# One instead of many: biases of an attention block carried by the first channel of the normalised rows, and an output bias moved from TensorE to GpSimd

## The chip, the cores and the metric

The kernel runs on one core of one Trainium2 chip. The metric is the device time of one execution in microseconds (us), the median of several runs. Beside these runs stands one execution under the hardware profiler, from which all durations of single instructions come.

## The reference

The input `x` is (4, 2048, 256) in float32: four sequences of 2048 tokens with 256 channels. Four blocks run one after the other, each on a layer norm (without gain or shift) of the current `x`, each adding its result to `x`:

```
x = x + broadcast over t of (norm(x)[:, 1] @ W.T + b)        # one row for a sequence
x = x + ffn(norm(x))                                           # token shift, W_k, relu^2, W_v, sigmoid gate
x = x + attention(norm(x))                                     # 16 heads of 64, blocks of 128, band mask
x = x + ffn(norm(x))                                           # the same weights as before
```

The attention projects `q`, `k`, `v` as `norm(x) @ W.T + bias`, turns `q` and `k` by their position, lets every block of 128 tokens look at itself and the block before it, and projects the result as `merged @ Wo.T + bo`. The biases `bq`, `bk`, `bv` and `bo` are not zero; they are what the change is about.

## The kernel before

The tokens are cut into 32 groups of 256 (`GB` = 2 blocks of 128), eight groups for each sequence. For each group the steps are: `Load` (load `x`, add the row of the first block), `Ffn` 0, `Ln` (layer norm for the attention, split into two float16 parts, transposed by DMA), `Val` and four `Qk` (projections, four heads at a time), four `Att` (scores, softmax, context), `Out` (output projection, added to `x`), `Ffn` 1, `Store`. Float32 precision is kept by splitting operands in a high and a low part and multiplying three times.

Each step has a line in a `SPEC` table: name, engine (`p` TensorE, `v` VectorE, `s` ScalarE, `g` GpSimd, `q` the DMA queue of SyncE), assumed duration, needed steps, buffers taken and given back. `Plan.order` plays these through with one queue for each engine: among the steps that could begin within `SLACK` (0.3 us) of the earliest, the one of lowest rank goes next. A rank is 44 us times the group plus an entry of the table `RANK` for the kind of step; the first and last five groups have further entries (`x!0`, `ln!-1`). The order so found is the program order of every engine, and an engine runs strictly in it. So a number in `RANK` moves instructions of one engine past each other without changing what they compute.

The places around the change:

- `Stats.scale` (on GpSimd) makes the two columns `rs` of a layer norm from mean and variance. For the attention's `Ln` it takes `shift = var * scale - mean`, so that `(x + shift) * scale` is the norm **plus one in every channel**. `Ln.xn` applies it on GpSimd; `Ln.hi` (ScalarE) and `Ln.lo` (GpSimd) make the two float16 parts.
- `Setup.fetch` builds the projection weights that go with this. The normalised row sums to zero over its channels, so each weight column may be shifted by a constant. Into a PSUM bank of 512 columns go: the matrix `less` (identity minus 1/256) times one half of the weights, `nones` (-1/256) times the other half, and four matmuls of `spread` that add the bias over 256 to every row. So the column sums to the bias, and "norm plus one" times it is the projection with its bias. This runs for q, k and v, for two halves of the channels (`wq0`, `wq1`, ...) and two banks each: 12 banks. `scale`, `hi` and `low` (VectorE, ScalarE, VectorE) then write the two float16 parts of the weights.
- `Setup.ob` (ten small GpSimd instructions) splits `bo` into three bfloat16 rows, `bo3`. In `Out.mm` every output bank half ends with one matmul of `ones` by `bo3`, which adds `bo` to the 24 matmuls of the projection: two for each group, 64 in all. `Out.add` on VectorE adds the bank to `x`.

The small biases are loaded by three DMAs of ScalarE's queue (`lb`); nearly all other DMAs go through SyncE's queue.

Of the kernel before, what the change touches and what calls it, by code (L numbers as in the profile page):

```python
# [8 lines left out]
BF16 = mybir.dt.bfloat16  # L9
# [9 lines left out]
P = 128  # L19
# [32 lines left out]
    "p.c1": -5056.91, "p.c2": 2969.02, "p.c3": -4885.05, "p.lv": -3111.05, "p.lb": -2925.83, "p.lw": -5009.81,  # L52
    "p.lo": -413.49, "p.lk": -2678.25, "p.lm": 2640.67, "p.lq": -3077.55, "p.fk": -1972.19, "p.fr": -2838.78,
    "p.fv": -777.00, "p.bd": -2779.47, "p.nvs": 3014.63, "p.nvm": 3072.90, "p.nvr": -2978.83, "p.nks": -788.22,
    "p.nkm": -4306.80, "p.nkr": -83.63, "p.nqs": -5037.35, "p.nqm": -4939.68, "p.nqr": -774.36, "p.sc": -472.11,
    "p.wv0": 570.16, "p.xv0": -201.89, "p.yv0": 3153.22, "p.zv0": -4686.76, "p.wv1": -2600.05, "p.xv1": -3342.91,
    "p.yv1": -610.29, "p.zv1": -4852.83, "p.wk0": -3021.86, "p.xk0": -1892.46, "p.yk0": -821.64, "p.zk0": -2369.83,
    "p.wk1": -2733.80, "p.xk1": -83.69, "p.yk1": -1953.56, "p.zk1": -2430.55, "p.wq0": -168.05, "p.xq0": 2297.47,
    "p.yq0": -4898.14, "p.zq0": -5081.41, "p.wq1": 2689.14, "p.xq1": -2913.52, "p.yq1": 3363.58, "p.zq1": -5071.63,
    "p.mk": -3071.43, "p.mu": -2906.24, "p.frh": -2530.67, "p.frl": -2423.55, "p.fkh": -2983.12, "p.fkl": 3185.31,  # L60
    "p.fvs": -769.81, "p.fvh": -4579.58, "p.fvl": 3091.15, "p.oq": -3006.79, "p.om": -204.90, "p.oc": -4648.57,
    "p.ox": -4580.42, "p.ob": -4965.08, "p.wo0": -613.03, "p.yo0": -2788.56, "p.zo0": -2882.62, "p.wo1": 3475.98,
    "p.yo1": -4703.07, "p.zo1": -4980.00, "r.ld": -5200.49, "r.st": 3455.58, "r.rs": -4687.73, "r.xn": 3456.91,
    "r.tr": 2907.19, "r.cp": -4814.90, "r.mm": 3513.18, "r.bi": -4976.56, "r.ad": -273.75, "x.ld": -4781.49,
    "x.a1": -513.94, "f0.st": -4882.63, "f0.rs": 2754.65, "f0.xn": 2986.21, "f0.tr": -4910.79, "f0.xt": -4990.79,
    "f0.hs": -3080.33, "f0.d": 2586.18, "f0.xm": -151.13, "f0.xo": -4611.65, "f0.xh": 976.57, "f0.xl": -4986.30,
    "f0.pk": -393.93, "f0.pr": -1868.76, "f0.rl": 3385.50, "f0.sq": 2308.38, "f0.kh": -5040.27, "f0.kl": -676.62,
    "f0.th": -6078.70, "f0.pv": 1034.70, "f0.sg": -4582.52, "f0.ad": 2796.64, "ln.st": -560.18, "ln.rs": -2135.71,
    "ln.xn": -358.88, "ln.hi": -845.47, "ln.lo": -4727.91, "ln.tr": -4597.42, "ln.cs": 1425.54, "tab.sc": 2955.10,
    "tab.st": -4548.65, "v0.mm": 1390.97, "v0.hi": -4851.14, "v0.lo": -952.76, "v1.mm": -2687.29,  # L70
    "v1.hi": -2644.64, "v1.lo": 2842.52, "v2.mm": 75.57, "v2.hi": -351.20, "v2.lo": -3081.42, "v3.mm": -4752.71,
    "v3.hi": -3057.25, "v3.lo": -4482.10, "q0.qm": -697.49, "q0.km": -1950.26, "q0.ka": -2699.89,
    "q0.kb": -5039.26, "q0.ad": 6.08, "q0.hi": -4974.92, "q0.lo": -5211.77, "q0.ks": -630.96, "q1.qm": -3584.31,
    "q1.km": -5189.02, "q1.ke": -5178.75, "q1.ka": -4943.18, "q1.mu": -992.72, "q1.ad": 1417.95, "q1.hi": 2888.04,
    "q1.lo": -4733.64, "q1.ks": -4326.00, "q2.qm": -468.39, "q2.km": -5058.89, "q2.ka": -2789.23,
    "q2.kb": -2972.37, "q2.ad": -2884.86, "q2.hi": 2658.83, "q2.lo": -924.24, "q2.ks": -2518.12, "q3.qm": 518.16,
    "q3.km": -4610.64, "q3.ka": 2530.62, "q3.kb": -4722.76, "q3.ad": -2764.39, "q3.hi": 2839.46, "q3.lo": -857.55,
    "q3.ks": -6086.78, "s0.k0": -1920.73, "s0.k1": -4586.15, "s0.k2": -613.21, "s0.k3": -2474.73,
    "s0.ks": -1923.23, "s0.sc": -3035.71, "s0.m0": -3099.45, "s0.m1": -3049.20, "s0.m2": -3015.22,
    "s0.m3": 2557.63, "s0.e0": -861.34, "s0.h0": -2876.34, "s0.l0": -2849.45, "s0.e1": 3370.73, "s0.h1": -2599.69,  # L80
    "s0.l1": 1349.23, "s0.t0": -2539.64, "s0.e2": 3083.70, "s0.h2": -1860.52, "s0.l2": 3055.36, "s0.e3": 2664.91,
    "s0.h3": -4879.42, "s0.l3": -610.50, "s0.t1": -4583.99, "s0.av": -4852.99, "s0.i0": 570.93, "s0.n0": -3079.20,
    "s0.ch": 2366.40, "s0.cl": -571.44, "s0.tc": -571.05, "s1.k0": -3309.12, "s1.k1": -1922.89, "s1.k2": -3002.20,
    "s1.k3": -2726.33, "s1.ks": -184.97, "s1.sc": -2823.37, "s1.m0": -2407.99, "s1.m1": -5176.15,
    "s1.m2": -1860.79, "s1.m3": 2664.46, "s1.e0": -2792.04, "s1.h0": -5036.68, "s1.l0": -5011.21,
    "s1.e1": -2759.97, "s1.h1": -2211.92, "s1.l1": -435.00, "s1.t0": -901.97, "s1.e2": 3228.18, "s1.h2": -2875.68,
    "s1.l2": -330.17, "s1.e3": -3095.98, "s1.h3": -4480.63, "s1.l3": -2400.51, "s1.t1": -40.32, "s1.av": -4976.07,
    "s1.i0": -302.67, "s1.n0": -5059.03, "s1.ch": -2945.71, "s1.cl": -4833.32, "s1.tc": -580.01, "s2.k0": -5104.06,
    "s2.k1": -2518.92, "s2.k2": -609.18, "s2.k3": -198.65, "s2.ks": -4270.64, "s2.sc": -3396.12, "s2.m0": -5359.90,
    "s2.m1": 3353.04, "s2.m2": -2954.66, "s2.m3": 2954.52, "s2.e0": -4801.17, "s2.h0": -4748.29, "s2.l0": -2533.65,  # L90
    "s2.e1": 2657.60, "s2.h1": -4876.22, "s2.l1": -143.77, "s2.t0": 3181.31, "s2.e2": -4740.23, "s2.h2": -1971.93,
    "s2.l2": -938.59, "s2.e3": 2929.40, "s2.h3": 3383.64, "s2.l3": -3250.26, "s2.t1": -4528.02, "s2.av": -3295.20,
    "s2.i0": -813.73, "s2.n0": -495.95, "s2.ch": -48.33, "s2.cl": 3091.26, "s2.tc": -696.74, "s3.k0": -677.40,
    "s3.k1": -3123.97, "s3.k2": -1933.84, "s3.k3": -465.00, "s3.ks": -4922.97, "s3.sc": -3446.85, "s3.m0": -798.61,
    "s3.m1": -4809.14, "s3.m2": 2876.12, "s3.m3": -4696.24, "s3.e0": -3417.38, "s3.h0": -4927.16,
    "s3.l0": -1999.52, "s3.e1": -4448.94, "s3.h1": -2880.18, "s3.l1": -280.82, "s3.t0": -2938.10,
    "s3.e2": -4878.66, "s3.h2": 3143.56, "s3.l2": -4964.39, "s3.e3": -4936.60, "s3.h3": -2514.89,
    "s3.l3": -1028.30, "s3.t1": -492.35, "s3.av": -2744.89, "s3.i0": 3016.46, "s3.n0": -1868.36, "s3.ch": 884.13,
    "s3.cl": -4564.07, "s3.tc": -5366.32, "o.o0": 2643.02, "o.o1": -3044.73, "o.ad": -158.89, "f1.st": 2937.82,
    "f1.rs": -2889.62, "f1.xn": 3469.38, "f1.tr": -4576.63, "f1.xt": 552.29, "f1.hs": -510.30, "f1.d": -2519.76,  # L100
    "f1.xm": 3150.42, "f1.xo": -608.94, "f1.xh": -2506.38, "f1.xl": -4708.72, "f1.pk": -1296.49, "f1.pr": 3476.81,
    "f1.rl": -5093.90, "f1.sq": -2850.79, "f1.kh": -5039.71, "f1.kl": -814.45, "f1.th": -3076.11, "f1.pv": 2685.28,
    "f1.sg": -2990.66, "f1.ad": -805.51, "sv.sv": -5172.96, "q0.kp": -272.05, "q1.kp": 3376.69, "q2.kp": -1225.68,
    "q3.kp": 3472.01, "o.b0": 1345.63, "o.b1": -2554.79, "w0.sv": 3471.29, "f2.st": -5011.19, "f2.rs": -3308.71,
    "f2.xn": -3405.13, "f2.tr": -2831.72, "f2.xt": -3325.07, "f2.hs": -2014.91, "f2.d": 1332.12, "f2.xm": 2950.21,
    "f2.xo": 2796.33, "f2.xh": 3364.00, "f2.xl": -909.62, "f2.pk": -2992.00, "f2.pr": 2885.42, "f2.rl": 539.64,
    "f2.sq": 1425.59, "f2.kh": -67.86, "f2.kl": 2844.93, "f2.th": 2905.43, "f2.pv": -5337.55, "f2.sg": 3157.44,
    "f2.ad": -4704.62, "w1.sv": 3214.41, "x!0": 280.61, "f0!0": -466.19, "ln!0": -1931.41, "tab!0": 407.32,
    "v0!0": -398.48, "v1!0": -330.74, "v2!0": -346.65, "v3!0": 347.03, "q0!0": -660.79, "q1!0": 28.80,
    "q2!0": 462.27, "q3!0": -379.97, "s0!0": 250.27, "s1!0": 1256.31, "s2!0": 655.38, "s3!0": -1508.73,  # L110
    "o!0": -1757.96, "f1!0": -2364.52, "sv!0": 2125.66, "x!1": -633.85, "f0!1": -1962.50, "ln!1": 1727.42,
    "tab!1": -240.15, "v0!1": -2055.69, "v1!1": -17.38, "v2!1": -1635.07, "v3!1": -1933.31, "q0!1": 1435.50,
    "q1!1": -913.86, "q2!1": 541.01, "q3!1": -1282.06, "s0!1": -1069.83, "s1!1": 856.98, "s2!1": -2363.56,
    "s3!1": -571.61, "o!1": 860.95, "f1!1": 519.89, "sv!1": -1291.03, "x!2": -877.71, "f0!2": -334.58,
# [1582 lines left out]
```

## Time and profile before

| what | value |
|---|---|
| median of three runs | 1602.65 us (1599.9 to 1604.53) |
| the profiled execution, its own time | 1597.72 us |
| span of its instructions | 1595.9 us |
| mean granted TensorE clock | 0.991 |
| instructions | 55776 |
| distance between the first and last output projection (`po`, groups 0 and 31) | 163.6 to 1574.8 us |

A view by groups gives, for each kind of instruction, its engine, output and inputs, the shape, the count, the busy time and the mean of one, and behind the last bar how long the engine was idle just before them and what ended that. A view by windows gives the busy time of every engine in a stretch of the span. The chain is the work that ended last, followed backwards: each piece is an instruction that nothing but the piece before it held up. All instructions carry line 276, the helper that records them, so they are told apart by their tiles: `u_q`, `u_k`, `u_v` are the banks of `fetch`, `po` that of `Out`, `a_*` belongs to `Ln`, `f_*` to `Ffn`, `at_*` to `Att`, `qk_*` to `Qk`. A matmul's duration includes its way through the array: where matmuls follow each other, the distance from start to start is what one costs.

### The profile page before, as it was taken

To read this page: it belongs to the slowest core of one execution; us is meant where nothing else is said; L and a number is where in the kernel's file an instruction comes from. 1 tells how busy PE (TensorE), PEld (TensorE's weight loads), DVE (VectorE), ACT (ScalarE), POOL (GpSimd) and SP (SyncE) were. 2 spreads that over 40 slices of the span, in tenths; PEclk is the share of its full clock that TensorE was granted. 3 is DMA by queue.
4 is the path that set the end of the run, shared out by engine and by line. 5 is a ranking of instruction groups with operands and counts; after the bars stand their busy time and mean duration, and the time that the engine had idled before them with its cause. 6 is when DMAs were issued, how large, how long until landed. Compare 5 with 4: busy or idle time off the path is not lost.

```text
span 1595.9 us, 55776 instructions
## 1 busy us (share of the span) xinstructions
PE 1493.1 (94%) x22887; PEld 1241.3 (78%) x22888; DVE 1438.1 (90%) x2607; ACT 1345.6 (84%) x2742; POOL 1317.3 (83%) x1409
## 2 busy tenths in 40 slices
PE   7989889999999999999999999999999999999976
PEld 4767778777777887887887878788887778887765
DVE  6889898999999999999999999999999999998973
ACT  5678788888988888898988889898888989888882
POOL 6899877788888888888888889888888988888732
PEclk9999999999999999999999999999999999999997
DMA  7059998889889799989798989997878989989781
GB/s 225 11 131 168 163 175 179 153 167 157 148 160 173 164 153 163 160 170 161 159 152 152 166 165 166 169 168 166 139 149 152 181 155 173 163 164 161 147 159 34
DMA packets 858831, 248.23 MB, mean 156 GB/s; under 512 B 822736, under 2 KB 857808, under 8 KB 858576
## 3 DMA queue, kind: packets, MB, share of 16 engines
q1 hardware_dynamic: 858144, 244.66, 82.3%
q8 instruction: 179, 2.93, 0.8%
q14 instruction: 76, 0.62, 0.1%
q10 hardware_dynamic: 432, 0.01, 0.0%
HBM read 42.22 MB, written 26.21 MB: 43 GB/s over the span
## 4 chain that ended last, share of the span: by engine, by line
PE 52%; DVE 18%; ACT 17%; POOL 7%; issue 6%; DMA 1%; DVEq 0%; ACTq 0%; SPq 0%; POOLq 0%
PE qk_pd L276 11%; PE po L276 9%; PE at_s L276 8%; PE pv L276 7%; PE at_cx L276 7%; PE f_pv L276 5%; ACT at_s L276 5%; DVE qk_A L276 3%; ACT at_phl L276 3%; DVE at_phl L276 3%; DVE at_mn L276 3%; PE f_pk L276 3%; PE f_pr L276 2%; DVE qk_B L276 2%; ACT f_xh L276 2%
## 5 line engine op out<-in xcount | busy, mean ns | idle before, releaser
L276 ACT ACTIVATE at_s<-at_s,at_mn 128x256 f32<-128x256 f32 x1024 | 462.7, 452 | 27.7 <-DVE at_mn L276 11.0
L276 DVE TENSOR_TENSOR at_phl<-at_s,at_phl 128x512 f16<-128x512 f32 x512 | 346.3, 682 | 40.3 <-ACT at_phl L276 37.1
L276 POOL TENSOR_TENSOR qk_A<-qk_A,qk_B 128x512 f32<-128x512 f32 x256 | 320.9, 1277 | 44.9 <-DVE qk_B L276 43.9
L276 DVE TENSOR_REDUCE at_mn<-at_s 128x2 f32<-128x512 f32 x512 | 325.3, 680 | 3.5 <-PE at_s L276 3.2
L276 ACT CAST at_phl<-at_s 128x512 f16<-128x512 f32 x512 | 300.6, 587 | 12.8 <-DMA at_pt<-at_phl 0.4
L276 PE MATMUL at_cx<-v,at_pt 128*128 128x65 f16 x5952 | 202.6, 194 | 37.3 <-DVE qk_B L276 24.5
L276 PEld LDWEIGHTS <-at_pt 128*128 128x128 f16 x5952 | 193.8, 98 | 52.0 <-issue 48.3
L276 POOL TENSOR_TENSOR at_ct<-at_c,at_ct 128x512 f16<-128x512 f32 x128 | 149.0, 1164 | 63.0 <-ACT at_ct L276 62.7
L276 PE MATMUL at_s<-qk_k,qk_q 32*128 32x256 f16 (+1 forms) x6144 | 189.7, 264 | 0.0
L276 PE MATMUL qk_pd<-a_xT,w_q_h 128*128 128x256 f16 x1024 | 176.3, 274 | 9.3 <-DVE at_c L276 3.8
L276 POOL TENSOR_TENSOR f_xl<-f_xm,f_xh 128x1024 fp32r<-128x1024 f32 x63 | 148.7, 2360 | 40.0 <-issue 24.9
L276 PE MATMUL po<-wo_h,at_ctT 128*128 128x256 f16 x1024 | 178.0, 273 | 1.0 <-DMA at_ctT<-at_ct 1.0
L276 DVE TENSOR_TENSOR qk_A<-qk_pd,a_cs 128x1024 f32<-128x1024 f32 x128 | 156.0, 1219 | 23.6 <-PE qk_pd L276 10.1
L276 PE MATMUL qk_pd<-a_xT,w_k_h 128*128 128x256 f16 x1024 | 176.8, 275 | 0.0
L276 PE MATMUL pv<-w_v_h,a_xT 128*128 128x512 f16 x512 | 161.7, 379 | 12.2 <-DVE at_phl L276 9.4
L276 PEld LDWEIGHTS <-at_ctT 128*128 128x128 f16 x1536 | 147.9, 98 | 18.1 <-DMA at_ctT<-at_ct 1.2
L276 PEld LDWEIGHTS <-qk_q 32*128 32x128 f16 x6144 | 153.4, 93 | 6.1
L276 POOL TENSOR_TENSOR qk_k<-qk_A,qk_k 128x512 f16<-128x512 f32 x128 | 149.4, 1167 | 0.0
L276 POOL TENSOR_TENSOR qk_q<-qk_A,qk_q 128x512 f16<-128x512 f32 x128 | 149.3, 1166 | 0.0
L276 PEld LDWEIGHTS <-a_xT 128*128 128x128 f16 x768 | 71.3, 98 | 98.9 <-DVE at_phl L276 16.9
L276 PE MATMUL qk_pd<-a_xT,w_k_l 128*128 128x256 f16 x512 | 140.6, 275 | 0.0
L276 PE MATMUL qk_pd<-a_xT,w_q_l 128*128 128x256 f16 x512 | 140.1, 274 | 0.0
(195 smaller groups left out, 3866.6 us busy)
## 6 DMA issues: line engine op xcount, KB each, us to landing
qk_kd<-qk_k SPq DMA_DIRECT2D x112, 128.0 KB, 2.4
qk_k<-qk_kd SPq DMA_DIRECT2D x112, 128.0 KB, 3.1
a_cs<-csd SPq DMA_DIRECT2D x24, 384.0 KB, 3.8
x<-in_x_dram SPq DMA_DIRECT2D x32, 256.0 KB, 3.6
out_dram<-x SPq DMA_DIRECT2D x31, 256.0 KB, 2.5
at_pt<-at_phl SPq DMA_TRANSPOSE x256, 4.5
a_cs<-in_cs_dram SPq DMA_DIRECT2D x32, 96.0 KB, 3.4
csd<-a_cs SPq DMA_DIRECT2D x8, 384.0 KB, 3.2
```

The costliest lines, as they stand in the source:

```text
L276: ins = fn(*a, **k)
```

## The change

Only the first channel of the norm gets one added. `Stats.scale` loses its special form for GpSimd (`shift` is now minus the mean for it), and `Ln.xn` adds one to channel 0 of both blocks with one more small GpSimd instruction. To match, every row of a weight column is shifted by the bias less the first weight, `b - w[0]`: row 0 then is the bias itself, and as the norm sums to zero the shift has no other effect. `fetch` does it with two matmuls for a bank: the identity times the weights, and a product of two rows (`sgn`: +1, -1) with two rows of a new tile `ends`: the bias and the first weight row. `ends` is loaded by the new step `lr`, six DMAs of ScalarE's queue; the bias has to be put in the order of the weights' columns, so its row is gathered in pieces of one element (4 bytes). `less`, `nones` and the bias over 256 go; `sgn` is made by three small GpSimd instructions.

`ob`, `bo3` and the two `po` matmuls by `ones` go. `bo` is loaded, in its own step `lx`, to a tile that stays (`bo_sb`), and a new step `Ln.bo` on GpSimd adds it to the group's `x` after the norm was taken; `Out.add` needs it. 

All numbers of `RANK` differ (515 entries before, 517 after: `p.ob` is gone, `ln.bo`, `p.lx` and `p.lr` are new), and some assumed durations in the tables. The new kinds rank `p.lr` -4235.42, `p.lx` -1399.37, `ln.bo` +3506.29; the other numbers are left out here.

```diff
@@ RANK @@
-    "p.c1": -5056.91, "p.c2": 2969.02, "p.c3": -4885.05, ...
+    "p.c1": -1400.22, "p.c2": -1269.16, "p.c3": -5785.06, ...
...
@@ Stats.scale @@
             g.tensor_tensor(scale, var, mhalf[:, :nb], op=ALU.pow)
-            if e is g:
-                g.tensor_tensor(shift, var, scale, op=ALU.mult)
-                g.tensor_tensor(shift, shift, mean, op=ALU.subtract)
-                return
             g.tensor_scalar(shift, mean, -1.0, None, op0=ALU.mult)
@@ Setup, the table @@
+        lr s 2.8 | lb            | phl>rw         |
-        lm q1 .9 |             | pt>tmp         |
+        lm q.5 .45 |           | pt>tmp         |
+        lx q.5 .45 |           |                |
-        wv0 p 5.45 | lv bd c3 c2 nvm | pair>uv0 | v0 v1
+        wv0 p 3.76 | lv lr c3 nvm | pair>uv0 | v0 v1 rw
...
-        ob g 7.5   | ox c1 mk    |                | tmp small
@@ Setup @@
-            nc.vector.memset(bo3, 0.0)
-            nc.vector.memset(nones, -1.0 / C)
         def c3(self):
-            nc.gpsimd.tensor_scalar(less, ident, -1.0 / C, None, op0=ALU.add)
+            g = nc.gpsimd
+            g.tensor_tensor(sgn, ident[:, 0:1], ident[:, 32:33], op=ALU.add)
+            g.tensor_tensor(sgn, sgn, ident[:, 64:65], op=ALU.add)
+            g.tensor_scalar(sgn, sgn, 2.0, -1.0, op0=ALU.mult, op1=ALU.add)
+        def lr(self):
+            self.ends = work("phl", [P, NH * HD], F32, "ends")
+            for i, (w, b) in enumerate(((wv, bv), (wk, bk), (wq, bq))):
+                row = self.ends[32 * i : 32 * i + 1, :]
+                nc.scalar.dma_start(row.rearrange("o (c p) -> o c p", p=P), b.rearrange("(o p) c -> o c p", o=1))
+                nc.scalar.dma_start(self.ends[32 * i + 1 : 32 * i + 2, :], w[0:1, :])
         def bd(self):
-            nc.gpsimd.tensor_scalar(self.bias, self.bias, 1.0 / C, None, op0=ALU.mult)
+        def lx(self):
+            nc.sync.dma_start(bo_sb[:, 0, :], bo.rearrange("(o c) -> o c", o=1).broadcast_to([P, C]))
         def fetch(self, nm, k):
             for hf, u in enumerate(self.u[nm, k]):
-                w = [W[nm][i][:, 0, hf * 512 : (hf + 1) * 512] for i in range(2)]
-                nc.tensor.matmul(u, less, w[k], start=True, stop=False)
-                nc.tensor.matmul(u, nones.broadcast_to([P, P]), w[1 - k], start=False, stop=False)
-                self.spread(u, self.bm[nm], ident, hf)
+                c = slice(hf * 512, (hf + 1) * 512)
+                nc.tensor.matmul(u, ident, W[nm][k][:, 0, c], start=True, stop=False)
+                e = slice(32 * "vkq".index(nm), 32 * "vkq".index(nm) + 2)
+                nc.tensor.matmul(u, sgn[e].broadcast_to([2, P]), self.ends[e, c], start=False, stop=True)
-        def ob(self):
...
@@ Ln @@
-        rs g 1.6  | st    |         |
-        xn g 1.06 | rs    | xn>xn   | mv rs
+        rs g 1.3  | st    |         |
+        xn g 1.36 | rs    | xn>xn   | mv rs
+        bo g 1.24 | xn p:lx |       |
         def xn(self):
             self.s.apply(nc.gpsimd, self.x, XT[self.g])
+            first = self.x[:, :, 0:1]
+            nc.gpsimd.tensor_scalar(first, first, 1.0, None, op0=ALU.add)
+        def bo(self):
+            x = XT[self.g]
+            nc.gpsimd.tensor_tensor(x, x, bo_sb.broadcast_to([P, GB, C]), op=ALU.add)
@@ Out @@
-        ad v .79  | o1           |        | po
+        ad v .79  | o1 ln:bo     |        | po
-                    stop=False,
+                    stop=(n == 23),
-            nc.tensor.matmul(PO[self.g][:, j, :], ones, bo3, start=False, stop=True)
```

## The prediction, as put on record before the result

> **What bounds the kernel now.** I read the busy shares first, then the windows for the setup and for one group, then the chain of waits, then single instructions. The page gives:
>
> ```profile
> PE 1493.1 (94%) x22887; PEld 1241.3 (78%) x22888; DVE 1438.1 (90%) x2607; ACT 1345.6 (84%) x2742; POOL 1317.3 (83%) x1409
> PE 52%; DVE 18%; ACT 17%; POOL 7%; issue 6%; DMA 1%; DVEq 0%; ACTq 0%; SPq 0%; POOLq 0%
> ```
>
> The first line is busy time, the second the chain's shares. TensorE leads in both. The shares mix stages, so I split by windows (columns: busy PE, PEld, DVE, ACT, POOL, each with its count, then clock and DMA):
>
> ```profile
> 12.00:62.00 50.00, 49.44 (x270) 33.26 (x269) 42.79 (x111) 32.77 (x68) 39.98 (x71) 1.00 0.38 119
> 100.00:160.00 60.00, 52.16 (x858) 43.41 (x861) 52.96 (x87) 52.22 (x107) 54.93 (x51) 1.00 0.83 163
> 752.00:799.00 47.00, 45.69 (x719) 38.32 (x718) 44.50 (x81) 41.88 (x86) 40.57 (x43) 1.00 0.69 147
> ```
>
> In the **setup** (12 to 62 us) TensorE is busy 49.4 of 50 us, with weight building and the first `Ffn` steps; the first attention projection starts at 63.66 us. TensorE sets the pace. In the **ramp** (100 to 160) GpSimd is the fullest, 54.9 of 60. In the **loop** one group takes 47.0 us, the distance at which the same instructions come back in the chain. There TensorE has 45.7, VectorE 44.5, ScalarE 41.9, GpSimd 40.6 us of work; nobody is full, and the chain decides. One turn of it (start, duration, what):
>
> ```profile
> 750.42 2.76 PE pv L276 x12
> ...
> 759.28 1.47 PE at_cx L276 x48
> 760.75 2.73 PE po L276 x25
> 763.47 0.44 PE f_pt L276 x4
> 763.91 2.73 PE po L276 x25
> ...
> 775.60 1.42 PE f_pr L276 x12
> ```
>
> From 750.42 to 777.01 it stays on TensorE without a gap (26.6 of the 47 us), and both output projections lie in it; the rest is ScalarE and VectorE. GpSimd is not in this turn.
>
> **The weights in the setup.** One bank of `fetch`:
>
> ```profile
> 25.33 1.02 PE L276 MATMUL u_k<-wk_sb,less 128*128 128x512 f32 x2
> 26.19 1.02 PE L276 MATMUL u_k<-wk_sb,nones 128*128 128x512 f32 x2
> 27.05 1.05 PE L276 MATMUL u_k<-ident,small 128*128 128x128 f32 x8
> 27.94 0.60 PE L276 MATMUL f_pt<-ident,f_xn 128*128 128x128 f32 x4
> ```
>
> From start to start: 0.86 (`less`), 0.86 (`nones`), 0.89 (four of `spread`); together 2.61 us. After the change a bank has the identity product, which the trace has in `u_o` (two full banks in 1.80 us, 33.80 to 35.60, so 0.90), and the product of two rows, which it does not have. That one streams the same 512 float32 columns as `nones`, so 0.86 is its upper end; its lower end is nothing. I take 0.86, the nearest row: two rows spare weight rows, not columns. So a bank goes from 2.61 to 1.76, and 12 banks save 12 x 0.85 = 10.2 us (upper bound, with the second product at nothing, 12 x 1.71 = 20.5), on an engine that has no gap there. What was next late: `ob` runs on GpSimd from 38.19 to 45.80 us and holds back the row statistics of the next `Ffn` (the chain goes through it). It goes too, 7.6 us, so GpSimd does not keep the old time. Against it, GpSimd loses `less` (0.57) and one bias scaling (0.30) and gets three small ones (some 0.25 each): nothing. Two VectorE memsets (0.17, 0.06) go.
>
> **The row load.** `lr` adds six DMA issues on ScalarE's queue, at 0.40 to 0.46 each (rows of the three bias loads) some 2.6 us. ScalarE waits from 3.4 to 8.45 us for `wv` anyway, so they are hidden; without that cover they would cost their 2.6. What they move is the doubtful thing: three times 1024 pieces of 4 bytes. The page:
>
> ```profile
> q1 hardware_dynamic: 858144, 244.66, 82.3%
> q10 hardware_dynamic: 432, 0.01, 0.0%
> ```
>
> The first queue's packets are mostly tiny: 0.823 x 16 x 1595.9 us / 858144 = 24.5 ns each. Those of ScalarE's queue took under 0.05%, so under 30 ns each. 3072 packets are 75 us of DMA engine time: 4.7 us if spread over 16 engines, 75 if on one. Issued by about 5 us, with the 3.7 to 4.9 us that the bias loads took to land, the rows are there between 14 and 85 us. The first `fetch` began at 14.77. The row nearest in kind, the bias loads (also 4 KB on this queue, in small pieces), landed without delay, so I take the early end and charge 1 us. The Trainium skill, "DMA: Bandwidth & Descriptors", section "Why a DMA increments its semaphore by 16 and not by 1", speaks against the best case: a copy runs on the largest number of engines up to 16 that divides the slowest dimension of both sides. That dimension is 8 here, so by it, as an estimate, the 75 us would be 9.4, the rows would land near 19 us, and the charge would be up to 4 us, not 1.
>
> **Output bias off TensorE.** In each half:
>
> ```profile
> 763.09 0.27 PE L276 MATMUL po<-wo_h,at_ctT 128*128 128x256 f16 x1
> 763.20 0.27 PE L276 MATMUL po<-bo,ones 128*128 128x256 bf16 x1
> 763.31 0.60 PE L276 MATMUL f_pt<-ident,f_xn 128*128 128x128 f32 x4
> ```
>
> It costs 0.11 us from start to start, not its 0.27. 64 of them: 7.0 us. As both halves stand in the turn of the chain, I take all of it; the other end is nothing, if another engine's part of the turn is late at once (VectorE has 44.5 us a group).
>
> **Output bias onto GpSimd.** The same shape with the same broadcast is in the trace, the first block's row added to `x`:
>
> ```profile
> L276 POOL TENSOR_TENSOR x<-x,vb 128x512 f32<-128x512 f32 x32 | 40.7, 1274 | 5.3 <-DVE vb L276 4.3 <-DMA x<-in_x_dram 1.0
> ```
>
> 32 x 1.274 = 40.8 us. In the norm two column instructions of 0.197 go, one of 0.24 and one of about 0.22 (first channel) come: +0.07 a group, 2 us in all, and the norm's latency is as before. So GpSimd goes from 40.6 to some 41.9 us of a group's 47. It fits, in gaps that are short (0.6 to 1.4 us in the timeline of GpSimd); a busy GpSimd does not yield, so where the add meets a ready instruction, that waits up to 1.27. Bounds: 0 and +40.8. GpSimd has 7% of the chain; I charge 7% of the 42.8, +3.0. The Trainium skill, "GPSIMD Engine Reference", section 4.1 "Engine selection", would have an elementwise add on VectorE, about twice as fast; the trace agrees in the ratio (`f_xl` with 512 columns takes 0.69 on VectorE). By that rule the add would save 0.6 a time, but on the engine with 44.5 of 47 us, where I would charge far more of it.
>
> The add of the bank to `x` (VectorE) now also waits for this GpSimd add. Queued behind it on VectorE are the score subtractions that release TensorE's banks. The cover is long: group 0's norm is applied at 57.7 us, its `po` is added at 166.8.
>
> **The order.** Every rank changed. Its price cannot be read from rows; a bound can: from `po` to `po`, the first six groups came 45.7 us apart (163.63 to 437.58), fourteen later ones 46.4 (763.20 to 1412.48). 0.7 us for 31 groups is 22 us either way. I take 0 and keep both ends.
>
> **Sum** in the profiled execution: -10.2 + 1.0 - 7.0 + 3.0 = -13.2, from 1597.72 to 1584.5 us. The median of the runs is 4.9 above that execution, so **1589 us**.
>
> **Rivals.**
> - *Spent on the way (within 0.3%).* Either the row load lands late or the ramp, where GpSimd is full, takes back the setup's gain. It decides when the rows land after about 25 us (14.8 + 10.2). Then only the loop's -7.0 + 3.0 is left: 1599. For it: 4-byte pieces, and 54.9 of 60 us in the ramp; against: `ob` is gone, and most of the pieces' time is spread.
> - *GpSimd in the turn (slower).* The bias add, ranked last of its group, starts in a gap just before an urgent step (`qk_A`, `f_xl`, the statistics). If that happens in the turn of every group it costs 1.27 x 31 = +39, less 17 of gain: 1625. It decides from some 44% of the groups on (17.2 / 39.4). For it: gaps hardly longer than the add; against: GpSimd is absent from the turn and has over 5 us of slack.
> - *Denser order.* The new ranks use what was freed and the loop goes at the first groups' pace: 22 us more, 1567.
>
> **How the numbers follow.** Forecast (1575 to 1598) 0.55; denser 0.13; spent 0.15; slower 0.17. A measurement of this kernel tells about 0.3% (5 us) from no change. So faster 0.68, same 0.15, slower 0.17. The range reaches from 1566, with half of the denser case, to 1610, the mild part of the slower one; outside it is about 0.19.
>
> **What would show it.** First attention projection (`qk_pd`) near 54 us instead of 63.66; banks 1.7 us apart; first `fetch` by 16 us. `po` with 24 matmuls in 2.6 us; period 46.8 or below. GpSimd near 42 us a group and still under 10% of the chain. I am wrong if `u_*` waits for the DMA `ends`, if the period grows above 47, or if GpSimd's share of the chain is over 15%.

## The result: 1.6% slower, and the profile after

The changed kernel took 1628.04 us, the median of four runs (1626.15 to 1629.84), against 1602.6 us of the kernel before: a ratio of 1.016 with a 95% interval of 1.0141 to 1.0179. Instead of 13 us fewer it takes 25 more. The profiled execution took 1629.84 us with a span of 1628.0, and the time after its last instruction is as before, so the span holds the whole loss. The two profiled executions lie 32.1 us apart in their spans, 6.7 more than the medians, so what is counted in the profiles below adds up to 32, not to 25.

The page of the changed kernel, with the busy line, the packets of ScalarE's DMA queue and the shares of the chain:

```profile
PE 1497.8 (92%) x22728; PEld 1225.6 (75%) x22728; DVE 1444.3 (89%) x2605; ACT 1337.4 (82%) x2742; POOL 1352.7 (83%) x1432
...
q10 hardware_dynamic: 3534, 0.04, 0.2%
...
PE 30%; DVE 22%; POOL 19%; ACT 17%; issue 7%; DMA 4%; ACTq 0%; SPq 0%; POOLq 0%; DVEq 0%
```

TensorE has 159 matmul records fewer and yet 4.7 us more of busy time. The 3102 new packets are the 4-byte pieces and rows. TensorE's share of the chain falls from 52% to 30%, and what it lost went to GpSimd, VectorE and DMA.

The setup comes first in time. The timeline of ScalarE (start, duration, what; ACTq is its queue issuing a DMA):

```profile
2.16 1.28 ACTq L277 DMA_DIRECT2D ends<-in_bv_dram  x1
5.20 2.33 ACTq L277 DMA_DIRECT2D ends<-in_wv_dram  x1
...
8.94 4.84 ACTq L277 DMA_DIRECT2D ends<-in_wk_dram  x1
...
17.45 4.87 ACTq L277 DMA_DIRECT2D ends<-in_wq_dram  x1
22.34 1.28 ACT L277 ACT_TABLE_LOAD   x1 [22.34 <-issue]
```

Six issues that I had put at 2.6 us take 14.7 (the two left out 0.69 and 0.68), with gaps between them, and ScalarE does no work of its own before 22.34 us. The costly ones are the loads of plain rows, each issued behind a load in pieces: 2.33, 4.84 and 4.87 us. In the changed kernel with contiguous rows (below) the same row takes

```profile
7.86 0.23 ACTq L277 DMA_DIRECT2D ends<-in_wk_dram  x1
```

so it is the load in pieces ahead of it that holds the issue up. The chain of the changed kernel runs through these loads:

```profile
5.20 11.51 DMA ends<-in_wv_dram
...
16.73 0.68 ACTq L277
...
17.45 4.87 ACTq L277
...
22.34 1.28 ACT L277
```

The first `fetch` starts at 27.78 us (before: 14.77), the first attention projection at 82.62 (before: 63.66). The banks are not 1.76 us apart either. One of them on TensorE, and the start of the next:

```profile
56.54 1.10 PE L277 MATMUL u_k<-wk_sb,ident 128*128 128x512 f32 x2
57.58 1.12 PE L277 MATMUL u_k<-ends,sgn 2*128 2x512 f32 x2
58.62 1.13 PE L277 MATMUL u_k<-wk_sb,ident 128*128 128x512 f32 x2
```

From start to start a product costs 1.04 us (elsewhere up to 1.06) where 128-row products behind each other cost 0.86, so a bank takes 2.08 to 2.10 us.

Taking the first `po` add of each group as the mark, the changed kernel is behind by 14.4 us at group 0 (181.2 against 166.8), 17.8 at group 1, 20.8 at group 4, 27.5 at group 24 and 32.0 at group 31. So about two thirds of it come with the setup and the ramp, some 7 us creep in over the loop, and 4.5 come in the last groups. The loop in the same window as before (busy PE, PEld, DVE, ACT, POOL, clock, DMA share):

```profile
752.00:799.00 47.00, 45.32 (x717) 37.87 (x717) 43.95 (x79) 41.00 (x86) 42.24 (x44) 1.00 0.95 158
```

GpSimd went up by 1.7 us, about as forecast, and all 32 adds together have one row:

```profile
L277 POOL TENSOR_TENSOR x<-x,bo_sb x32: 1257/1278/1298, 77.0 to 1510.7; 128x512 f32<-128x512 f32 x32
```

(least, median and greatest ns of one). Under it the view names nobody who waited for such an add.

### The profile page after: what moved, and what is told of

It reads as the page before. It is cut to its first block, busy times and chain, and to the rows that moved or that the text cites. A ratio compares the mean times of both kernels' runs of the same rounds, so it can differ in the third digit from the quotient of the medians.

```text
span 1628.0 us, 55486 instructions
## 1 busy us (share of the span) xinstructions
PE 1497.8 (92%) x22728; PEld 1225.6 (75%) x22728; DVE 1444.3 (89%) x2605; ACT 1337.4 (82%) x2742; POOL 1352.7 (83%) x1432
## 4 chain that ended last, share of the span: by engine, by line
PE 30%; DVE 22%; POOL 19%; ACT 17%; issue 7%; DMA 4%; ACTq 0%; SPq 0%; POOLq 0%; DVEq 0%
PE qk_pd L277 7%; PE po L277 5%; ACT at_s L277 5%; POOL qk_A L277 4%; DVE qk_A L277 4%; DVE at_phl L277 4%; PE pv L277 4%; PE at_s L277 3%; PE at_cx L277 3%; ACT at_phl L277 3%; DVE at_mn L277 3%; DVE f_xm L277 2%; POOL at_ct L277 2%; POOL x L277 2%; PE f_pk L277 2%
## 5 line engine op out<-in xcount | busy, mean ns | idle before, releaser
L277 ACT ACTIVATE at_s<-at_s,at_mn 128x256 f32<-128x256 f32 x1024 | 463.0, 452 | 37.6 <-DVE at_mn L277 20.8
L277 POOL TENSOR_TENSOR qk_A<-qk_A,qk_B 128x512 f32<-128x512 f32 x256 | 320.7, 1275 | 32.9 <-DVE qk_B L277 32.1
L277 PE MATMUL pv<-w_v_h,a_xT 128*128 128x512 f16 x512 | 169.7, 379 | 15.6 <-DVE f_kl L277 9.4
```

Of the source, the lines that this page charges most:

```text
L277: ins = fn(*a, **k)
```

## The experiments

All ratios are to the kernel before, run beside it on the same chip, with 95% intervals. "Old order" means that the rank table and the table of steps of the kernel before are kept, so that every untouched instruction stays at its place.

### What in the new order can be taken away

**Contiguous rows** (`rows_contiguous`): the bias row comes from a DRAM input that holds it in the right order.

```diff
-                nc.scalar.dma_start(row.rearrange("o (c p) -> o c p", p=P), b.rearrange("(o p) c -> o c p", o=1))
+                nc.scalar.dma_start(row, brow[i : i + 1, :])
```

> The changed kernel, but the three bias rows come from DRAM already in the order of the weights' columns (a 4 KB contiguous row each), not as 1024 pieces of 4 bytes; same ranks, same issuing queue. Theory L (late rows: the pieces hold ScalarE's queue until 22.3 us and move the first attention projection from 63.7 to 82.6 us, and the end keeps most of it): ScalarE's first square before 12 us, first projection at 62 to 70 us, time 1608 to 1617. Rival G (the output bias add on GpSimd lengthens the loop) and rival O (the new order does): the ramp swallows the setup, time 1622 to 1629.

1622.99 us, 1.0132 (1.0106 to 1.0158): 5 us less by the medians (the intervals overlap), where theory L had 1608 to 1617 and its rivals 1622 to 1629. ScalarE is free at 9.57 us and the first `fetch` starts at 15.82, but the first `qk_pd` still comes at 77.6, 14 us later than before. The windows of this kernel show why TensorE did not use its start:

```profile
24.00:28.00 4.00, 4.00 (x14) 1.51 (x14) 2.58 (x9) 1.41 (x3) 2.29 (x9) 0.76 1.03 335
...
32.00:36.00 4.00, 4.00 (x5) 0.99 (x5) 3.90 (x6) 3.76 (x8) 3.77 (x6) 0.50 0.28 92
36.00:40.00 4.00, 4.00 (x5) 0.99 (x5) 3.83 (x6) 0.34 (x1) 3.85 (x5) 0.50 0.54 164
```

TensorE is "busy" for the whole of the last two windows and does five matmuls in each: the granted clock is 0.50. "Busy" here is a bank that takes 4 us instead of 1.76.

**No bias add** (`no_bias_add`): the step stays, its GpSimd instruction goes, so the output lacks `bo`.

> The changed kernel without the GpSimd add of the output bias (that part of the computation is left out: the output lacks it); the step keeps its place in the plan, so the order is the same. Rival G: the loop falls back by 0.35 us a group or more, 1628 goes to 1600 to 1620. Theories L and O: GpSimd had room for it, 1624 to 1628.

1629.0 us, 1.018 (1.0159 to 1.0201): the same as with the add, and rival G fell. GpSimd's share of the chain falls to 9%, the time does not. GpSimd's add costs nothing here that the runs can tell, and a share of the chain is not a price.

**Whole-tile products in the new order** (`new_order_full_rows`): contiguous rows, and the two rows lie in a zero-filled tile of which all 128 rows are multiplied.

```diff
-                nc.tensor.matmul(u, sgn[e].broadcast_to([2, P]), self.ends[e, c], start=False, stop=True)
+                nc.tensor.matmul(u, sgn[:, i : i + 1].broadcast_to([P, P]), self.ends[:, c], start=False, stop=True)
```

> The changed kernel in its own order, with contiguous bias rows and the product over all 128 rows of a zero-filled tile. Beside the same with two rows (1623.0, first qk_pd 77.6, granted clock 0.50 from 28 to 48 us). Theory C: clock 0.99 or more from 20 to 60 us, banks 1.75 us apart, first qk_pd 66 to 73, 1612 to 1619 us. If the setup is held by another engine there, the first qk_pd stays within 2 us of 77.6 and the time at 1621 to 1625.

1621.08 us, 1.012 (1.0105 to 1.0135), first `qk_pd` at 74.6. Banks are 1.75 us again, 3 us are gained at the first projection, 2 in the end (the intervals overlap). The clock still falls (0.84 and 0.74 from 28 to 36 us, 0.54 at 44), now behind stretches in which TensorE waits. So the price of the two-row form is small, and theory C (that two-row products cost more than whole tiles and pull the clock down) is only a part.

**64 matmuls put back** (`new_order_64_matmuls`): `ones` by a tile of zeros, where the bias was added before; the sum is unchanged.

```diff
-                    stop=(n == 23),
+                    stop=False,
                 )
+            nc.tensor.matmul(PO[self.g][:, j, :], ones, bo3, start=False, stop=True)
```

> The changed kernel in its own order, with 64 matmuls of ones by a tile of zeros put back where the output bias was added on TensorE (the sum is unchanged by them). If the turn of the groups still lies on TensorE there, as the prediction took it, they cost their 7.0 us: 1635. Theory T (in the new order the turn goes through VectorE, ScalarE and GpSimd instead, so that TensorE's saving buys nothing): 0 to 3 us, 1628 to 1631.

1637.31 us, 1.0222 (1.0206 to 1.0237): 9 us more than the changed kernel by the medians, 5 between the two profiled executions. My theory T fell. TensorE's saving is worth about its 7 us in the new order too; it is simply outweighed.

### The order

**Rank tables exchanged** (`changed_old_ranks`: the changed code with the numbers of the table before, and the three new kinds as they are; `before_new_ranks`: the reverse, with rank 0 for `ob`, which the new table lacks).

> The changed kernel with the rank table of the kernel before (the three new kinds keep their new ranks). Rival O (the new order is the worse one): at or below 1615. L and G: the order is not the matter, 1623 to 1635.

> The kernel before with the rank table of the changed one (the bias split step, which that table does not have, gets rank 0). Rival O: 1615 or more. L and G: within 1597 to 1610, as neither the row load nor the GpSimd add is in it.

1856.2 us (1.1593, 1.1547 to 1.1639) and 1781.02 us (1.1121, 1.1104 to 1.1137). A table fits only the steps and assumed durations for which it was found, and so the exchange does not separate code from order. It does show how far an order can move the time of one and the same code: by 178 us for the kernel before and by 228 for the changed one, where I had allowed 22.

**The whole change in the old order** (`old_order_whole_change`): all edits of the change, issued at the places of what they replace.

> The order of the kernel before with the whole change as written: bias rows in 4-byte pieces on ScalarE's queue, product of two rows, first channel, output bias on GpSimd. If the parts add (1.0101 and 0.9962 of 1600.7), it is 1611 us. Theory O says that the rest up to the changed kernel's 1628 (some 17 us) is the new order: this kernel at 1606 to 1614. If the code alone makes the loss and the order none, it is 1625 or more.

1611.43 us, 1.0058 (1.0043 to 1.0073). It is also what the parts measured one by one below add up to (1611). This is the experiment that divides the loss: the code alone costs 9 us, and the new order the other 16.6 (19.9 between the two profiled executions). The order loses them in the loop and the last groups; at group 0 the two are only 2 us apart. From the `po` add of group 0 to that of group 24 the same code takes 1108.7 us in the old order (179.2 to 1287.9) and 1122.9 in the new (181.2 to 1304.0), 0.59 us a group; another 4.9 come from there to group 31. In the chain of the old order one still finds the run on TensorE that set the pace before:

```profile
764.02 2.77 PE pv L276 x12
766.78 2.62 PE qk_pd L276 x24
...
774.35 2.62 PE po L276 x24
776.97 0.44 PE f_pt L276 x4
777.40 2.62 PE po L276 x24
```

In the new order the chain leaves TensorE in the stretch shown and is handed through ScalarE, VectorE and GpSimd:

```profile
938.82 1.44 PE f_pr L277 x12
940.31 0.47 issue
940.78 1.04 ACT f_xh L277
...
961.40 1.21 DVE v L277 x2
962.61 0.63 ACT at_ct L277
963.31 1.16 POOL at_ct L277
964.46 2.45 POOL qk_A L277 x2
```

Which single step costs the 0.59 us is not shown; no run moved one rank alone.

### The parts of the change in the old order

**Bias add on GpSimd alone** (`old_order_bias_add`): the split of `bo` and the 64 matmuls go, `bo_sb` and this line at the end of `Ln.lo` come.

```diff
+            x = XT[self.g]
+            nc.gpsimd.tensor_tensor(x, x, bo_sb.broadcast_to([P, GB, C]), op=ALU.add)
```

> The kernel before, its order kept, with one part of the change: the output bias is added to x by GpSimd at the end of the group's low-part instruction, and the 64 matmuls by ones and the split of bo are gone. The prediction's terms (-7.0 us off TensorE, +3.0 on GpSimd) give 1594 to 1602 us. If GpSimd's add stands in the turn of the groups (theory G) it is 1615 or more, and the share of GpSimd in the chain rises from 7% to over 12%. Theory O (the new order lost the time, not the code) agrees with the first.

1594.35 us, 0.9962 (0.995 to 0.9975). This beats both kernels. It is 6.3 us less, near the prediction's -4.0 for these two terms and within the 1594 to 1602 expected. In the profile the first group comes 2.3 us later (169.1), and then 0.22 us a group is saved.

**The row loads alone** (`old_order_pieces_alone`): the kernel before plus the six loads of the change into a tile that nobody reads.

> The kernel before, nothing changed but that the six row loads of the change (the bias in 4-byte pieces) are issued in the bias step on ScalarE's queue, into a tile that nobody reads. The prediction charged 1.0 us for them: 1603. Theory L (they hold up ScalarE's own queue, and SyncE's queue waits for them in turn): 1612 to 1620, ScalarE's first work near 22 us, SyncE waits over 10 us for DMA ends, and most of the 17 us that the kernel with rows in pieces lost is here.

1612.8 us, 1.0065 (1.0052 to 1.0079): 10.8 us for six loads that move 24 KB for nobody. The waits of SyncE's queue in the first 60 us (total, times, longest):

```profile
SPq L276 <- DMA ends<-in_wk_dram: 4.1, 1, 4.1
SPq L276 <- DMA ends<-in_wv_dram: 3.3, 1, 3.3
...
SPq L276 <- DMA ends<-in_bv_dram: 2.7, 1, 2.7
```

SyncE's queue, which issues none of these loads, stands 14.7 us for them (2.3, 1.8 and 0.5 for the three that are not shown): its loads wait for loads of another queue before they are issued. In all, its waits for DMAs in these 60 us grow from 13.4 to 24.5. So what SyncE loads is late too, not only what ScalarE computes.

**New weights in the old order, in three forms**: as written (`old_order_rows_in_pieces`), with contiguous rows (`old_order_two_rows`), and with whole-tile products as well (`old_order_full_rows`). The output bias stays on TensorE in all three.

> The kernel before, its order kept, with the other part of the change: first channel plus one, weight banks by the identity and a product of two rows, and the six row loads on ScalarE's queue with the bias in pieces of 4 bytes; the output bias stays on TensorE. The prediction's terms (-10.2 + 1.0) give 1593 us. Theory L (the pieces hold up ScalarE's queue by some 15 us and the banks come later) gives 1605 to 1618, ScalarE's first work near 22 us, and the first qk_pd 5 us or more after 63.7.

> As the kernel with rows in pieces, but the three bias rows come from a DRAM input that holds them in the right order, so that each is one contiguous row. Theory L alone: the loss is gone, banks 1.76 us, 1593 us. Theory C (the product of two rows costs 1.05 instead of 0.86, and TensorE loses clock while such products run): banks 2.1 us at full clock and up to 4.2 at half clock, granted clock below 0.9 somewhere before 62 us, 1597 to 1612 us.

> As the kernel with two rows, but the second product runs over all 128 rows of a zero-filled tile that holds the two rows, with columns of a signed selection as weights. Theory C: banks 1.75 us apart, granted clock 0.99 or more in the setup, 1590 to 1595 us, and at least 4 us below the kernel with two rows. If the row load or the first channel's extra instruction costs the time, it is no faster than the kernel with two rows.

1617.63 us (1.0101, 1.0087 to 1.0115), 1604.3 (1.0022, 1.0013 to 1.0031) and 1606.88 (1.0035, 1.0023 to 1.0048). Pieces cost 13 us over contiguous rows. But even the last form, whose first banks are 1.7 us apart, is not faster than before; I had expected 1590 to 1595. Its TensorE shows where the saving goes:

```profile
27.98 1.02 PE L276 MATMUL u_k<-ends,sgn 128*128 128x512 f32 x2
35.27 0.35 PE L276 MATMUL pm<-small,ones 128*128 128x1 bf16 x8 [6.27 <-POOL small L276]
35.48 3.76 PE L276 MATMUL u_o<-wo_sb,ident 128*128 128x512 f32 x4
```

The first six banks are done 4.6 us sooner, and then TensorE waits 6.27 us for GpSimd's `small`, the last product of its block of masks. After the wait the clock is 0.50, and `u_o` takes 3.76 us instead of 1.96.

**Both parts, and one obstacle after the other taken away**: whole-tile and two-row products together with the bias add (`old_order_all_full_rows`, `old_order_all_two_rows`), then one load of six rows instead of six loads (`old_order_one_row_load`), then also the mask loaded early on ScalarE's queue (`old_order_early_mask`).

> The order of the kernel before; contiguous bias rows, product over all 128 rows, first channel, output bias on GpSimd (the split of bo gone). Each part alone left the first qk_pd at 63.7 or later. Theory P (two paths of nearly the same length through the setup: TensorE's banks, and GpSimd with the split of bo and the row statistics; shortening one alone gains nothing): with both shortened the first qk_pd comes at 57 to 62 us and the time is 1586 to 1594. If the parts only add (+6.2 and -6.3): 1600 to 1601, first qk_pd near 66.

> As the kernel with all parts and full rows, but with the product of two rows. Adding the parts: 1598. Theory P with theory C (TensorE at half clock and 2.1 us banks while the two-row products run): first qk_pd 62 to 66, 1592 to 1599, so behind the full-row kernel by 2 us or more.

> As the kernel with all parts and full rows in the old order (1605.2), but the six rows come in one DMA of six contiguous rows from a DRAM input laid out so, on partitions 0 to 5. Theory M (the extra loads push the mask and so GpSimd's mask block back; with it in time only the first half of the banks is hidden behind that block): the mask lands within 1 us of 25.7 us, first qk_pd 57 to 61 us, 1586 to 1594. If the row loads are not what is late: 1603 to 1607, first qk_pd 66 to 67.

> As the kernel with one row load, and the mask is loaded on ScalarE's queue ahead of the rows into a tile of its own, so that GpSimd's mask block waits for no load. Theory M: first qk_pd another 1 to 3 us earlier than with one row load, 1584 to 1592. If GpSimd's mask block is not the late one, it is the same as with one row load within 1 us.

1605.16 us (1.0015, 1.0005 to 1.0026), 1603.66 (1.0017, 1.0005 to 1.0029), 1603.24 (1.0002, 0.9993 to 1.0011) and 1602.22 (1.0004, 0.9995 to 1.0013). Theories P and M both fell by their times; only the 1 to 3 us that M forecast from the early mask came (2.4). The two-row form is not behind whole tiles here. The first `qk_pd` came at 67.1, 66.9, 65.1 and 62.75 us: with all of these taken away 0.9 us before the old 63.66, not 5 to 10. The chain of the last one through the setup says what is left:

```profile
31.91 0.17 POOL small L276
...
32.76 3.62 PE u_o L276 x4
36.38 4.19 PE u_q L276 x8
...
45.96 2.37 POOL f_xl L276
...
56.05 1.11 POOL a_xn L276 x2
...
60.24 0.70 DVE f_kl L276
60.98 1.96 PE f_pv L276 x10
```

Between 44 and 61 us it never touches TensorE. In that stretch lie four of the six later banks, so their saving is worth nothing, and the first six end in the wait for `small`, which lasts 4.61 us even here; `u_o` behind it takes 3.6 us of the chain instead of 1.8.

**The first channel** (`old_order_first_channel_alone`: the bias add in the old order plus the small instruction, adding zero; `old_order_no_first_channel`: the early-mask kernel without it, whose output lacks the biases of q, k and v).

> The kernel with the bias add in the old order (1594.35, ratio 0.9962), with the added small GpSimd instruction on the first channel of the norm after it was applied; it adds zero, so nothing changes in the output. The prediction charged 0.07 us a group for this exchange. Theory R (in the ramp the instruction stands in the path of the norm, and the ramp loses what the loop does not show): 1598 to 1602, ratio 0.998 to 1.0, with the distance from the first qk_pd to the third po add over 203 us. Otherwise it stays at 1593 to 1596, that distance at 199 to 201.

> The kernel with one row load and the early mask, without the instruction that adds one to the first channel; its output lacks the biases of q, k and v. Theory R: 1593 to 1598, first qk_pd at 62.4, from there to the third po add 199 to 202 us. If the ramp's loss comes from the way the setup ends (idle TensorE, clock), it stays at 1600 to 1603 and that distance above 204.

1597.13 us (0.997, 0.9959 to 0.9981) and 1600.79 (0.9995, 0.9986 to 1.0004). The instruction costs some 1 to 3 us (the intervals with and without it overlap), nearly all in the first two groups: from the first `qk_pd` to the third `po` add it is 202.4 us instead of 199.8. Taking it out of the other kernel leaves that distance at 209.4. Theory R fell.

## Why the prediction was wrong, step by step

**"TensorE sets the pace" in the setup: the step that failed.** I read it from 49.4 busy microseconds of 50. The chain of the kernel before for the same stretch says something else:

```profile
34.63 2.35 POOL f_xl L276
36.98 1.23 POOL x L276
38.20 0.46 POOL tmp L276
...
45.01 0.72 POOL bo L276
...
47.43 2.31 POOL f_xl L276
...
61.62 0.70 DVE f_kl L276
62.37 1.44 PE f_pv L276 x10
```

It runs on GpSimd from 27 to 51 us, but for waits of some hundredths, and then through ScalarE and VectorE. I even noted that the chain goes through `ob`, and counted TensorE's saving all the same. With the bias add alone, which removes `ob`, the chain of the same stretch is TensorE's up to 56.4 us (then, as before, ScalarE's and VectorE's), and ends at the same microsecond:

```profile
28.50 5.22 PE u_k L276 x24
...
35.83 5.46 PE u_q L276 x24
...
51.19 5.23 PE u_v L276 x24
...
62.38 1.44 PE f_pv L276 x10
```

So at least two paths of nearly one length lead to the first projection: dropping 7.6 us from the one moved it by nothing, and taking up to 10 us of work off the other as well moved it by about 1 us at best, and in three kernels made it later. "An engine that has no gap there" is true of TensorE and does not make its work the end of anything.

**Banks, -10.2 us.** The identity product at 0.86 to 0.9 is right for whole tiles. The two-row product is 1.05, above what I had called its upper end of 0.86; a bank is 2.10, not 1.76, and TensorE's saving 6.1 instead of 10.2. The bound failed since it was taken from products of one shape behind each other. Whole-tile products mixed with each other cost 0.86 here as well, so the 0.19 goes with the change between 128 and 2 rows. A weight load of that length (0.18 us in the view of `ends`) lies hidden between equal shapes; that it comes into the open is what the row spacing suggests, not what a run isolated. In all, new weights and first channel cost about +6 us (17.0 in pieces less 10.8 of the loads alone) instead of -10.2; with contiguous rows it is 3.6, loads included.

**Row load, +1.0 us: 10.8.** I worked out when the rows land, and asked nothing about the queue that issues them. "ScalarE waits from 3.4 to 8.45 us for `wv` anyway, so they are hidden" took 0.40 to 0.46 us an issue from the bias loads, which are 4 KB as well but not single elements: three of them make 432 packets, and the six new loads 3102. And the cost to SyncE's queue was not asked for at all, though the waits of before show that queue standing for a load that ScalarE's queue had issued:

```profile
SPq L276 <- DMA small<-in_bq_dram: 1.3, 1, 1.3
```

The Trainium skill, "DMA: Bandwidth & Descriptors", section "Why a DMA increments its semaphore by 16 and not by 1", had led the prediction to an estimate of up to 4 us: nearer, but also about the landing alone. The Trainium skill, "Perfetto Trace Analysis", section 'What "DMA-bound" means', names the sequencer of the issuing engine as a place of its own where DMAs bind, and puts the size of the pieces first there; 14.7 us of issue for 24 KB agree with that.

**Output bias off TensorE, -7.0, and onto GpSimd, +3.0: right in the main.** Together -4.0; alone in the old order 6.3 less by the medians. In the profiles it is 2.3 more by group 0 and 7.0 less from there to group 31, so the -7.0 is met, and the +3.0, which I had taken from a share of the chain, agrees by luck at best: in the new order the add costs nothing. 64 matmuls put back in the new order cost 5 to 9.

**First channel, +2 us in all:** measured 1 to 3.

**The order, 0 with 22 either way: +16.6.** Inside the bounds, and I should have left it less near zero: every other term was worked out on the placement of before, and the new one keeps none of it. The six fast groups from which I took the bound and the "denser" rival belong to the ramp: the `po` adds there come 49.5, 47.0, 39.8, 44.0, 47.0 and 47.0 us apart, two short distances behind a long one and not a pace.

These terms add up: +10.8 for the loads, +6.2 for the weights and first channel, -6.3 for the bias make 10.7 (9.1 measured together), and 16.6 for the order.

**The rivals.** "GpSimd in the turn" had the right sign and nearly the time, 1625, for a wrong reason: without the add the time is the same. "Spent on the way" was right that the setup's gain is taken back, but put the point at the landing of the rows; it was taken back even with the rows in time, and its time, 1599, was 29 us short. Of what I had named as signs, `po` with 24 matmuls in 2.62 us and GpSimd at 42.2 us came true, the period stayed below 47 on the mean (46.8), and GpSimd's share of the chain (19%) passed my mark of 15% without being the cause.

**What stays open.** Which steps of the new order cost 0.59 us a group. And why every kernel with the new weights loses another 2 to 6 us at group 2 in the old order (49 to 53 us from the `po` add before, instead of 47): between 224 and 248 us the granted clock falls to 0.50 to 0.85 in all of them, in or behind a window of 6 us in which TensorE waits, and is 1.00 in the kernel before and in the two with the bias add and the old weights. The first channel is not the cause. Nor does it take the new weights: the kernel before with nothing but the six loads added shows it too (48.6 us, clock 0.77). What the cause is was not tried.

## What to carry to other kernels

A busy engine is a bound only where the chain runs on it: before an edit is given its full price, follow the chain of the same stretch, and ask which other path ends within a microsecond or two. An added DMA can be paid on the queue that issues it and on another queue that waits for it, as here, so a gather in 4-byte pieces in a setup wants a layout that makes it one row. And where a change brings a new order with it, measure the code in the old order: here one part of the change alone, at the old places, is 0.4% faster than the kernel before, and the whole in its own order 1.6% slower.

## What the runs showed of the hardware

- A load of 1024 pieces of 4 bytes holds up its queue: the issue behind it takes 2.3 to 4.9 us in the changed kernel, against 0.23 for the same row behind a contiguous load.
- A float32 product over 2 rows, in turn with products over 128 rows, costs 1.05 us for 512 columns at full clock (the trace has two records for it); over 128 zero-filled rows 0.86. The narrower product is the slower one.
- The granted clock falls to 0.50 while TensorE counts as busy all the time. With two-row products in the new order and contiguous rows it fell to 0.76 in the window from 24 to 28 us, with no wait of TensorE's since 11.4 us (the next is 1.10 us, at 28.5), and stayed at 0.50 to 48 us. It need not: in the old order (`old_order_two_rows`) the same products ran at 1.05 us and a clock of 1.00 from 29 to 57 us. There, from 15 to 23 us, they took 2.0 us each although the row gives 1.00, so the row does not show every slow stretch. With whole tiles in the old order the clock fell behind waits of 4.5 to 6.7 us and made the two banks of `u_o` take 3.55 to 3.76 us instead of 1.96. The Trainium skill, "TensorE: Matmul & The Clock Gate", Part 1, says that an idle window of about 3.4 us halves the clock. These waits agree with it; in `new_order_full_rows` the clock fell (0.84, then 0.74) behind a wait of 3.14 us, which is a little less; and the fall with two-row products is not covered by it, as there was no idle window.
